# A new issue order for two Sobel layers, and the centring of recurrent weights spread one step to a pair

## The chip, the cores and the metric

The kernel runs on one core of a Trainium2 chip. The core has five engines that run side by side, each with its own queue of instructions that it takes strictly in order: TensorE (PE, matrix products), VectorE (DVE), ScalarE (ACT), GpSimd (POOL) and SyncE (SP, which here only issues transfers). An instruction waits at the head of its queue until semaphores say that what it needs is there. The metric is the device time of one execution in microseconds (us); the median of several executions counts.

## The reference

The input is one image of 256 x 256 pixels with 32 channels, and four layers follow each other, each of the form x = x + f(GroupNorm(x)), with 16 groups over the whole image:

1. an attention over an axis of length one, so that its softmax is 1 and only value, gate and output projection count;
2. and 3. a Sobel layer: a 3x3 mean of the normalized image with zero padding, divided by the number of pixels in the window, then the two Sobel gradients of it, and their magnitude;
4. two recurrent cells over the 256 columns, with a group norm in each step.

```python
pooled = _avg_pool3_same(x)
grad_x = _depthwise3(pooled, kx)
grad_y = _depthwise3(pooled, ky)
return jnp.sqrt(grad_x * grad_x + grad_y * grad_y + EPSILON)
```

Layers 2 and 3 are what the change is about. The recurrent layer comes in through its weights, which are prepared while the Sobel layers run.

## The kernel before

**Layout.** The image lies in SBUF twice, as `xa` and `xb`, each of 128 partitions (4 columns x 32 channels) by 64 blocks by 256 rows. Two blocks make a pair: 128 x 512 numbers. There are 32 pairs (`NST`). A layer reads one image and writes the other, pair by pair.

**One pair of a Sobel layer** (`sobel_layer`, from L382). Work along the free axis (the image's rows) is done by VectorE and GpSimd; work across columns, which means across partitions and neighbouring blocks, is done by matrix products with constant matrices.

- `convert` (L407, ACT, twice): the normalized pair, once into PSUM (`xp`) and once into SBUF (`xn`).
- `twos` (L412, DVE): u, the sum of neighbours, from `xn` and `xp`. `ends` (L417, ACT): the two border values of `pp`, from u times 1.5. `threes` (L422, DVE): the rest of `pp`, the sum of three, from u (SBUF) and `xp` (PSUM). `pp` has two buffers.
- `fours` (L426, DVE): v, the sum of `pp` and `pp` shifted by one. Both operands lie in SBUF.
- `difference` (L435, POOL): dh, `pp` minus `pp` shifted by two. `smooth` (L431, POOL): sh, the sum of v and v shifted by one. Both go into rings of eight blocks (four pairs), since the products need the neighbouring pairs as well.
- `mixed` (L439, PE, twice): for dh and for sh, four products into PSUM, two on each half of the columns; the pair before and the pair after are needed.
- `square` (L473, ACT, twice), `total` (L479, DVE: ss), `root` (L483, ACT), `residual` (L487, DVE: adds the magnitude to the layer's input and writes its output), `statistics` (L490, DVE: bn_stats of the output, for the next group norm).

**What sets the order.** The order of issue is written out by hand. The list `parts` (L494) gives each operation a time within its pair, in units of its own; pair k is moved by k times `every` (L493). All operations of all pairs are sorted by that number and issued in this order (`todo`, L512 to L518). So the numbers decide the order in each engine's queue, and nothing else: when an instruction really runs is up to the queues and semaphores. In steady state, VectorE's queue holds for each pair k: u(k), residual(k-4), statistics(k-4), pp(k), ss(k-3), v(k). ScalarE's: ends(k), the two squares of pair k-3, the two conversions of pair k+1, root(k-3). GpSimd's: dh(k), sh(k). PE's: the products of dh and then those of sh, two pairs behind.

**The work in between.** After each `statistics`, one function of a list is called (L519). In the first Sobel layer the list comes from `centring` (L612): the recurrent weights and biases get their means subtracted. That is two reductions on VectorE for the biases (`bm`), one scaling, eight subtractions on GpSimd (`bc`, L629), then four reductions for the weights (`wm`), one scaling and sixteen subtractions (`wc`): 32 steps. L634 binds them two and two, so that the first 16 pairs take them all. In the second layer the list comes from `products` (L636): a transposition with its copy on ScalarE, two copies on GpSimd, two additions into the biases on VectorE (L651) behind a matrix product each, and an output matrix `e4` with copies on ScalarE and an addition on GpSimd (L666). It has five steps and is not edited.

**Around the layers.** Between the layers the statistics are gathered and turned into a scale and a bias (`group_norm`). After the second Sobel layer the recurrence starts (from 631 us in the profile); SP loads its first inputs `xt` from `xa` as soon as the Sobel buffers are free.

Of the kernel before, what the change touches and what calls it, by code (L numbers as in the profile page):

```python
# [60 lines left out]
def net_kernel(  # L61
# [320 lines left out]
    def sobel_layer(src, dst, scale, bias, between):  # L382
# [107 lines left out]
        def statistics(k):  # L490
            nc.vector.bn_stats(stats[:, k, :], pair(dst, k))  # L491

        every = 3.65  # L493
        parts = [  # L494
            (-1.19, convert, ("xp",)),
            (-0.74, convert, ("xn",)),
            (0.00, twos, ()),
            (0.52, ends, ()),
            (1.98, threes, ()),
            (3.36, difference, ()),  # L500
            (3.62, fours, ()),
            (5.32, smooth, ()),
            (8.70, mixed, (1,)),
            (9.90, mixed, (0,)),
            (12.45, square, (1,)),
            (12.47, square, (0,)),
            (13.90, total, ()),
            (14.41, root, ()),
            (15.59, residual, ()),
            (16.31, statistics, ()),  # L510
        ]
        todo = [  # L512
            (k * every + when, k, part, args) for k in range(NST) for when, part, args in parts
# [8 lines left out]
        return stats  # L522

    stats = sobel_layer(xa, xb, *gn, rw.centring())
    with tc.tile_pool(name="ps_n", bufs=1, space=PSUM) as ps_n:
        gn = group_norm(stats, ps_n, 3, 12)
    stats = sobel_layer(xb, xa, *gn, rw.products())
    second.close()

# [39 lines left out]
class RecurrentWeights:  # L569
# [42 lines left out]
    def centring(self):  # L612
        nc = self.nc
        out = []
        for mean, t in (
            (self.bm, self.bc.rearrange("p l (g m) -> p (l g) m", g=4)),
            (self.wm, self.wc.rearrange("p l k (g m) -> p (l k g) m", g=4)),
        ):
            n = mean.shape[1]
            for i in range(0, n, 4):  # L620
                out.append(
                    lambda mean=mean, t=t, i=i: nc.vector.tensor_reduce(
                        mean[:, i : i + 4], t[:, i : i + 4, :], AX.X, ALU.add
                    )
                )
            out.append(lambda mean=mean: nc.vector.tensor_scalar_mul(mean, mean, 1.0 / H))
            for i in range(n):
                out.append(
                    lambda mean=mean, t=t, i=i: nc.gpsimd.tensor_scalar(  # L629
                        t[:, i, :], t[:, i, :], mean[:, i : i + 1], None, ALU.subtract  # L630
                    )
                )

        return [lambda ps, p=out[i : i + 2]: [f() for f in p] for i in range(0, len(out), 2)]  # L634

    def products(self):  # L636
        nc = self.nc
# [87 lines left out]
class RecurrentInputs:  # L725
# [33 lines left out]
    def of(self, t, rows):  # L759
# [20 lines left out]
        i=10.749, m=14.225, sq=14.912, rd=15.578, pw=16.964, si=17.174, so=17.198, tg=17.865,  # L780
# [3 lines left out]
        i=17.550, m=17.552, sq=18.681, rd=19.727, pw=20.540, si=20.935, sf=21.284, fc=21.803,  # L784
# [289 lines left out]
```

## Time and profile before

| what | us |
|---|---|
| median of 3 runs (2635.06 to 2637.7) | 2635.57 |
| the profiled execution's own time | 2633.51 |
| its span, first to last instruction | 2631.7 |
| first Sobel layer, first u to last statistics | 327.78 to 471.09 |
| second Sobel layer, likewise | 477.20 to 619.46 |
| first products of the recurrence | 631.3 |
| busy in the span: PE, DVE, ACT, POOL | 2553.0, 2348.0, 2291.8, 1273.7 |
| granted TensorE clock, mean | 0.991 |

The span of the profiled execution is 1.8 us shorter than its own time, and that is 2.1 us under the median. Almost nine tenths of the span belong to the recurrence and the first layer, so shares over the whole span say little about the Sobel layers; what they are worth is read from their own stretch. Rows of the timeline give start, duration, engine, line, operation, output from input, shape and count, and in brackets how long the engine had been idle and what ended that. Instructions of one engine may overlap a little: the next one on VectorE starts about 0.07 us before the one in front of it ends, so periods are counted from start to start. Rows of groups give the number of instructions, busy time, the mean duration in ns, and the idle time before them with its releasers.

### The profile page before, as it was taken

To read this page: it belongs to the slowest core of one execution; us is meant where nothing else is said; L and a number is where in the kernel's file an instruction comes from. 1 tells how busy PE (TensorE), PEld (TensorE's weight loads), DVE (VectorE), ACT (ScalarE), POOL (GpSimd) and SP (SyncE) were. 2 spreads that over 40 slices of the span, in tenths; PEclk is the share of its full clock that TensorE was granted. 3 is DMA by queue.
4 is the path that set the end of the run, shared out by engine and by line. 5 is a ranking of instruction groups with operands and counts; after the bars stand their busy time and mean duration, and the time that the engine had idled before them with its cause. 6 is when DMAs were issued, how large, how long until landed. Compare 5 with 4: busy or idle time off the path is not lost.

```text
span 2631.7 us, 43547 instructions
## 1 busy us (share of the span) xinstructions
PE 2553.0 (97%) x11453; PEld 1004.5 (38%) x11453; DVE 2348.0 (89%) x6735; ACT 2291.8 (87%) x6948; POOL 1273.7 (48%) x1288
## 2 busy tenths in 40 slices
PE   7999988987999999999999999999999999999997
PEld 4433433433333333333333333333333333333332
DVE  6788799896999999999999999999999999999996
ACT  5677677675999999999999999999999999999996
POOL 2211265442555555555555555555555555555553
PEclk9899999998999999999999999999999999999998
DMA  4000000002010000001010101010000001000000
GB/s 146 1 1 1 18 1 1 1 1 49 1 24 9 18 12 14 16 10 20 6 21 5 21 5 21 5 24 9 18 11 15 16 10 20 6 5 5 5 5 10
DMA packets 110745, 38.71 MB, mean 15 GB/s; under 512 B 74852, under 2 KB 107653, under 8 KB 110488
## 3 DMA queue, kind: packets, MB, share of 16 engines
q1 hardware_dynamic: 108452, 34.54, 6.1%
q8 instruction: 94, 1.54, 0.2%
q14 instruction: 163, 1.34, 0.2%
q10 hardware_dynamic: 1236, 0.99, 0.1%
q0 software_dynamic: 800, 0.30, 0.1%
HBM read 10.63 MB, written 8.39 MB: 7 GB/s over the span
## 4 chain that ended last, share of the span: by engine, by line
PE 86%; DVE 9%; ACT 2%; issue 1%; DMA 1%; POOL 1%; SPq 0%; DVEq 0%; ACTq 0%; POOLq 0%
PE zz L892 35%; PE zz L887 17%; PE zz L860 8%; PE pt L944 6%; PE pv L315 5%; PE zz L857 3%; DVE v L429 3%; PE pt L940 2%; PE pg L339 2%; DVE stats L491 2%; DVE u L415 1%; PE px L989 1%; PE pg L315 1%; DVE pp L424 1%; PE pc L259 1%
## 5 line engine op out<-in xcount | busy, mean ns | idle before, releaser
L908 POOL TENSOR_TENSOR rs<-ve,mhalf 128x4 f32<-128x4 f32 x1024 | 1046.9, 1022 | 954.6 <-DVE ve L905 954.6
L892 PE MATMUL zz<-wc,hT 128*128 128x512 f32 x2040 | 1068.7, 611 | 1.4 <-DVE hT L950 1.2
L881 ACT ACTIVATE ga<-zz,rs 128x128 f32<-128x128 f32 x3072 | 974.6, 376 | 53.0 <-POOL rs L908 46.3
L905 DVE TENSOR_REDUCE ve<-sq 128x4 f32<-128x516 f32 x1024 | 704.9, 688 | 68.0 <-ACT sq L900 47.4
L900 ACT ACTIVATE sq<-zz 128x512 f32<-128x512 f32 x1024 | 623.8, 609 | 52.2 <-PE zz L892 14.2
L887 PE MATMUL zz<-wc,hT 128*128 128x512 f32 x1024 | 524.1, 594 | 0.0
L892 PEld LDWEIGHTS zz<-wc,hT 128*128 128x128 f32 x2040 | 306.4, 189 | 356.1 <-DVE hT L950 167.5
L881 ACT ACTIVATE go<-zz,rs 128x128 f32<-128x128 f32 x1024 | 394.1, 385 | 0.0
L928 DVE TENSOR_TENSOR c<-ga 128x128 f32<-128x128 f32 x1024 | 298.2, 291 | 64.5 <-ACT ga L881 58.0
L932 DVE TENSOR_TENSOR fc<-ga,c 128x128 f32<-128x128 f32 x1020 | 297.9, 292 | 5.6 <-ACT ga L881 4.1
L936 DVE TENSOR_TENSOR c<-c,fc 128x128 f32<-128x128 f32 x1020 | 286.6, 281 | 8.8
L860 PE MATMUL zz<-fx,xt 32*128 32x512 f32 x2048 | 265.7, 588 | 0.0
L471 PE MATMUL pg<-dh,kt 128*64 128x512 f32 (+1 forms) x584 | 175.8, 544 | 24.9 <-POOL dh L437 24.6
L333 DVE TENSOR_TENSOR o<-pv,sg 128x512 f32<-128x512 f32 x256 | 158.0, 680 | 42.3 <-PE pg L315 37.7
L940 PEld LDWEIGHTS pt<-ident,go 128*128 128x128 f32 x512 | 71.1, 139 | 290.2 <-ACT go L881 282.7
L887 PEld LDWEIGHTS zz<-wc,hT 128*128 128x128 f32 x1024 | 172.6, 208 | 9.4 <-issue 9.4
L944 PEld LDWEIGHTS pt<-ident,c 128*128 128x128 f32 x512 | 71.1, 139 | 268.2 <-DVE c L936 260.1
L947 ACT ACTIVATE th<-c 128x128 f32<-128x128 f32 x512 | 165.9, 324 | 4.4 <-DVE c L936 1.2
L944 PE MATMUL pt<-ident,h 128*128 128x128 f32 x512 | 157.5, 308 | 10.4 <-DVE h L954 8.1
L330 ACT ACTIVATE sg<-pg 128x512 f32<-128x512 f32 x256 | 138.6, 599 | 30.0 <-PE pg L315 25.3
L947 ACT ACTIVATE th<-pt 128x128 f32<-128x128 f32 x512 | 146.3, 286 | 18.9 <-PE pt L944 18.9
L950 DVE TENSOR_TENSOR hT<-pt,th 128x128 f32<-128x128 f32 x512 | 144.1, 281 | 13.7 <-ACT th L947 13.7
(161 smaller groups left out, 3006.0 us busy)
## 6 DMA issues: line engine op xcount, KB each, us to landing
xt<-xa SPq DMA_DIRECT2D x256, 64.0 KB, 2.0
nat<-in_x_dram SPq DMA_DIRECT2D x16, 512.0 KB, 7.8
out_dram<-st SPq DMA_DIRECT2D x252, 32.0 KB, 1.7
wc<-in_L_conv_W_cell_dram SPq DMA_DIRECT2D x2, 512.0 KB, 5.0
kt<-in_consts_dram ACTq DMA_DIRECT2D x1, 832.0 KB, 5.8
wv<-in_L_conv_Wv_dram POOLq DMA_DIRECT2D x4, 32.0 KB, 5.0
wg<-in_L_conv_Wg_dram POOLq DMA_DIRECT2D x4, 32.0 KB, 6.7
out_dram<-st ACTq DMA_DIRECT2D x4, 32.0 KB, 3.8
```

The costliest lines, as they stand in the source:

```text
L860: nc.tensor.matmul(v["zz", l, h, t], lhsT=inputs.of(t, r), rhs=fx[r, :], start=False, stop=l == 0 and t == 0,)
L881: nc.scalar.activation(dst, gates(x, g), func, scale=scale)
L887: nc.tensor.matmul(get("zz"), lhsT=v["hT", 0, t][:, seqs], rhs=wc[:, l, 0, :], start=False, stop=t == 0)
L892: nc.tensor.matmul(get("zz"), lhsT=v["hT", l, t - 1][:, seqs], rhs=wc[:, l, 1, :], start=False, stop=True,)
L900: nc.scalar.activation(sqs[l, h][:, :, 0:H], four(get("zz")), AF.Square, scale=float(H**-0.5))
L905: nc.vector.tensor_reduce(ve, sqs[l, h], AX.X, ALU.add)
L908: nc.gpsimd.tensor_tensor(rs, get("ve"), inputs.mhalf, ALU.pow)
L928: nc.vector.tensor_mul(c, gates(get("ga"), 0), gates(get("ga"), 2))
L932: nc.vector.tensor_mul(fc, gates(get("ga"), 1), get("c"))
L936: nc.vector.tensor_add(c, c, get("fc"))
L944: nc.tensor.transpose(get("pt")[:, 1, 0:P], get("c" if turned else "h"), ident)
L947: nc.scalar.activation(th, get("pt")[:, 1, 0:P] if turned else get("c"), AF.Tanh)
```

## The change

Two edits. The list of times in `sobel_layer` gets other numbers. In steady state they give this order for pair k. VectorE: u(k), residual(k-4), pp(k), statistics(k-4), v(k), ss(k-3). ScalarE: ends(k), the two squares of pair k-3 in the other order (that of sh first), conversions of pair k+1, root(k-3). GpSimd: sh(k-1), the step in between if there is one, dh(k); in its queue that is dh and sh by turns as before. PE: the products of sh for pair k-2, then those of dh for pair k-1, by turns as before, those of dh one pair earlier. The work in between stands where statistics stands: now between statistics and v on VectorE, and between sh(k-1) and dh(k) on GpSimd. Which instruction waits for which result is as before. At a layer's start, where there is no residual and no statistics yet, v follows directly on pp, as before; only the fourth v now stands ahead of the first ss.

The second edit takes the steps of `centring` one by one: 32 steps for 32 pairs, the last of them after the last statistics.

```diff
-        every = 3.65
+        every = 3.55
         parts = [
-            (-1.19, convert, ("xp",)),
-            (-0.74, convert, ("xn",)),
+            (-2.19, convert, ("xp",)),
+            (-2.05, convert, ("xn",)),
             (0.00, twos, ()),
-            (0.52, ends, ()),
-            (1.98, threes, ()),
-            (3.36, difference, ()),
-            (3.62, fours, ()),
-            (5.32, smooth, ()),
-            (8.70, mixed, (1,)),
-            (9.90, mixed, (0,)),
-            (12.45, square, (1,)),
-            (12.47, square, (0,)),
-            (13.90, total, ()),
-            (14.41, root, ()),
-            (15.59, residual, ()),
-            (16.31, statistics, ()),
+            (0.23, ends, ()),
+            (1.36, threes, ()),
+            (2.12, fours, ()),
+            (2.54, difference, ()),
+            (4.61, smooth, ()),
+            (6.40, mixed, (1,)),
+            (8.63, mixed, (0,)),
+            (11.70, square, (0,)),
+            (11.94, square, (1,)),
+            (12.98, total, ()),
+            (14.18, root, ()),
+            (14.75, residual, ()),
+            (16.24, statistics, ()),
         ]
...
-        return [lambda ps, p=out[i : i + 2]: [f() for f in p] for i in range(0, len(out), 2)]
+        return [lambda ps, f=f: f() for f in out]
```

## Prediction

> **What bounds the kernel now.** I read the groups of instructions first, for what the Sobel layers' operations cost; then busy time by stretches, for the engine that bounds these layers; then the timeline of a few pairs, for the order of events; last the layer's end, where one chain stands bare.
>
> ```profile
> L429 DVE TENSOR_TENSOR v<-pp 128x514 f32<-128x514 f32 x64 | 74.3, 1161 | 0.7
> L437 POOL TENSOR_TENSOR dh<-pp 128x512 f32<-128x512 f32 x64 | 72.0, 1125 | 91.2 <-ACT xp L410 69.8 <-DVE pp L424 15.5 <-PE pg L471 5.9
> L433 POOL TENSOR_TENSOR sh<-v 128x512 f32<-128x512 f32 x64 | 66.4, 1038 | 37.5 <-DVE v L429 29.8 <-PE pg L471 7.6
> ...
> 520.00:560.00 40.00, 36.01 (x169) 12.95 (x167) 39.66 (x57) 29.43 (x57) 19.74 (x19) 1.00 0.00 1
> ```
>
> The sum v takes 1.16 us where VectorE's other operations of this size (u, pp, ss) take 0.67 to 0.68. The last row (columns PE, PEld, DVE, ACT, POOL) is from the middle of the second Sobel layer: VectorE is busy 39.66 of 40 us, PE 36.0 with overlaps counted, ScalarE 29.4, GpSimd 19.7. VectorE bounds both layers. One period of its work, in the timeline:
>
> ```profile
> 543.44 0.67 DVE L424 TENSOR_TENSOR pp<-u,xp 128x508 f32<-128x508 f32 x1
> ...
> 544.02 0.68 DVE L481 TENSOR_TENSOR ss<-sq,pg 128x512 f32<-128x512 f32 x1
> ...
> 544.28 1.04 POOL L437 TENSOR_TENSOR dh<-pp 128x512 f32<-128x512 f32 x1 [1.49 <-ACT xp L410]
> ...
> 544.62 1.25 DVE L429 TENSOR_TENSOR v<-pp 128x514 f32<-128x514 f32 x1
> ...
> 545.79 0.67 DVE L415 TENSOR_TENSOR u<-xn,xp 128x510 f32<-128x510 f32 x1
> ...
> 546.02 1.04 POOL L433 TENSOR_TENSOR sh<-v 128x512 f32<-128x512 f32 x1 [0.70 <-PE pg L471]
> ...
> 546.39 0.67 DVE L488 TENSOR_TENSOR xa<-xb,pg 128x512 f32<-128x512 f32 x1
> ...
> 547.10 0.69 DVE L491 BATCH_NORM_STATS2 stats<-xa 128x6 f32<-128x512 f32 x1
> ...
> 547.71 0.67 DVE L424 TENSOR_TENSOR pp<-u,xp 128x508 f32<-128x508 f32 x1
> ```
>
> From start to start: pp 0.58, ss 0.60, v 1.17, u 0.60, residual 0.71 (statistics wait for its result), statistics 0.61: 4.27 us a pair. The difference dh starts 0.84 after pp's start, that is as soon as pp is there; v comes 0.34 later, and ends 0.55 after dh does (545.87 against 545.32). So v waits for dh: 0.57 us a pair. At the layer's end nothing covers the chain from total over root to residual:
>
> ```profile
> 613.86 0.67 DVE L481 TENSOR_TENSOR ss<-sq,pg 128x512 f32<-128x512 f32 x1
> 614.57 0.69 ACT L485 ACTIVATE pg<-ss,sobel_eps 128x512 f32<-128x512 f32 x1 [1.07 <-DVE ss L481]
> ...
> 615.29 0.69 DVE L488 TENSOR_TENSOR xa<-xb,pg 128x512 f32<-128x512 f32 x1 [0.76 <-ACT pg L485]
> ```
>
> It is 1.43 us from ss to residual. In the old order v, u and 0.60 more lie between them (544.02 to 546.39, 2.37), so it costs nothing.
>
> **What the Trainium skill says.** "SBUF — State Buffer", section "Who interferes with whom": a VectorE instruction with two SBUF inputs contends with a GpSimd instruction that reads SBUF, whoever is first blocks the other, one with at most one SBUF input doesn't, and tensor_reduce never does. The trace agrees: v alone of these operations reads two SBUF operands, and v alone is stretched; u lies beside sh and takes 0.67. Of a tensor_reduce beside dh no row of before shows anything.
>
> **The change, step by step.** In steady state VectorE's new order is ss, u, residual, pp, statistics, v. dh still waits for pp, for the scaled ends on ScalarE and for an old ring slot on PE, all as before; on GpSimd's queue it still stands between the last pair's sh and its own, with at most one centring in front. Its being issued after v in the program doesn't hold it back, for v is on another queue. One period, with ss at 0:
> - u at 0.60. root at 0.71, residual at 1.43: only u lies between now, so VectorE waits 0.23 for ScalarE.
> - pp at 2.03 (0.60 on). Statistics at 2.62 (0.59); the residual is done by then, so the old 0.11 for it goes. v is issued at 3.23.
> - dh at pp + 0.84 = 2.87, to 3.91. v starts 0.36 after it, waits, ends at 3.91 + 0.55 = 4.46; the next ss starts 0.08 before that (545.79 against 545.87), at 4.38.
>
> With ss and root at 0.68 and 0.69 while other engines run, I take 4.39, against 4.27: +0.12. From the fifth pair on 27 periods in each layer: 54 x 0.12 = +6.5 us.
>
> Others follow. ScalarE (some 3.1 of 4.39), PE (two steps of 0.43 for each of four groups, 3.4) and GpSimd (1.04 + 1.04 + 0.60 for one centring) fit into the period. Had they not, their excess would be added in full.
> - The six means of the centring (reductions, 0.67) stood before pp and cost 0.59 each from start to start, the two scalings 0.08: 3.7. Now they stand between statistics and v: v is issued 0.59 later, ends at pp + 2.47 instead of 2.44, so each costs 0.04. But in the pair behind the first two, v took 0.68 before, which saved 0.57. Net 0.24 - 3.7 + 0.57 = -2.9. If a reduction doesn't overlap with dh this is zero.
> - Centring one to a pair: GpSimd had 0.34 idle even behind two (1.19), so nothing is won on the path. Four are left to the layer's last pairs, behind the last sh, where GpSimd has 4 us free; layer 2 needs them some 20 us later.
> - The layer's start: the first root is ready early, -0.2 in each.
> - Layer 2's products. Before, the six periods from u at 488.07 took 1.95 more than 6 x 4.27. After: the copy of the transposed weights now precedes root on ScalarE and waits for PE one group longer, +0.7; the two additions into bc, between statistics and v, cost 0.1 each; the addition into e on GpSimd now stands ahead of dh and waits for ScalarE's copies, so one v is free of dh (-0.6) and one partly (-0.3). Together about 0, so -2.0 (this takes in the start).
> - The tail: the last residuals start behind u + 4.39 + 0.83 instead of u + 4.27 on, +0.95 a layer.
>
> Layer 1: 3.2 - 2.9 - 0.2 + 0.95 = +1.0. Layer 2: 3.2 - 2.0 + 0.95 = +2.1. The recurrence, from 631 us on, is untouched; the loads of xt on SP (29 issued in 18.8 us, the first 16 needed by 631) start when PE lets go of the ring, move with the tail, and have 5 us to spare. No DMA changes its place. Sum +3.0 us: 2633.5 for the profiled execution becomes 2636.5, and the median of 2635.57, 0.08% above it, becomes 2638.6.
>
> **Rivals.** First, v gets ahead of dh. Three of the 64 pairs show it:
>
> ```profile
> 505.64 1.93 POOL L437 TENSOR_TENSOR dh<-pp 128x512 f32<-128x512 f32 x1 [1.89 <-DVE pp L424]
> 505.99 0.68 DVE L429 TENSOR_TENSOR v<-pp 128x514 f32<-128x514 f32 x1
> ```
>
> v starts 0.35 after dh, takes 0.68, and dh is stretched by 0.9 instead. These are the pairs with 0.353 to 0.355 between the starts; in those where v waits it is at most 0.347. The new order gives about 0.36. For: the distance. Against: a later start is an odd reason to win; all three stand right behind VectorE instructions on 33 partitions (the bm reductions, the additions into bc), which the normal pair has not; and in two pairs v started 0.05 after dh and waited the longest (1.54). If v wins everywhere, the period is 4.38 - 0.55 = 3.83, GpSimd (1.93 + 1.04 + 0.60 = 3.57) still fits: 54 x -0.44 = -23.8; the credit of the reductions goes (+0.6 against before), the products cost +0.5, tails +0.4 each, start -0.2: about -22, 2613.5. In layer 2 alone, where no centring shifts dh: about -10.
>
> Second, slower: the wait of residual for root. It stands on VectorE's queue ahead of pp, statistics and v, so PE and GpSimd get their inputs late with it. I have 0.24 a pair. The change is slower by over 0.2% (5.3 us) once it is 0.04 wider, since 54 x 0.043 = 2.3. ScalarE's root has the ends behind it and the conversions before it; if root starts 0.1 late in each pair, +5.4: 2644. Against: ScalarE idles a microsecond before root.
>
> Third, the change doesn't do what it says (v still beside dh): that is my forecast.
>
> **From cases to numbers.** v still waits for dh with the sum as worked out: 0.55, 2633 to 2644, of which 0.40 within 0.2%, 0.13 above, 0.02 below. v ahead, in both layers or one: 0.25. Wider wait, or credits that fail: 0.20. So faster 0.27, same 0.40, slower 0.33; 0.2% is about what a measurement of this kernel can tell from no change. The range runs from the first rival's time to just past the second's, 2612 to 2646.
>
> **What would show it.** v with a mean near 1.2 us, and dh at 1.04 beside it; an idle time before the residual of over 0.2 a pair released by root; 4.39 between two pp; reductions directly before v, with v near 0.7 there. A v of 0.68 with a dh of 1.93 in most pairs makes the first rival right, an idle time of 0.3 or more the second. The forecast falls too if tensor_reduce is stretched beside dh.

## The result, and the profile after

The changed kernel takes 2641.82 us (median; 2638.98 to 2645.66), the kernel before 2635.36 beside it (2634.1 to 2637.7). The ratio is 1.0024, interval 1.0014 to 1.0034: slower by 0.24%, or 6.5 us. 2638.6, 3.0 us more than the kernel before, was forecast.

| us | before | after | difference | forecast |
|---|---|---|---|---|
| first Sobel layer | 143.32 | 144.93 | +1.61 | +1.0 |
| second Sobel layer | 142.26 | 145.85 | +3.58 | +2.1 |
| from the second layer's end on | 2012.22 | 2014.66 | +2.4 | 0 |
| span of the profiled execution | 2631.7 | 2640.0 | +8.3 | +3.0 |

(The rest of the span differs by +0.7: -0.2 before the first layer, +0.84 between the two.) First the groups of the changed kernel, and its row for the middle of the second layer (columns PE, PEld, DVE, ACT, POOL):

```profile
L437 POOL TENSOR_TENSOR dh<-pp 128x512 f32<-128x512 f32 x64 | 70.8, 1106 | 94.5 <-DVE pp L424 54.8 <-ACT xp L410 19.2 <-PE pg L471 17.4
L429 DVE TENSOR_TENSOR v<-pp 128x514 f32<-128x514 f32 x64 | 69.0, 1078 | 0.9
...
520.00:560.00 40.00, 38.12 (x174) 14.65 (x170) 38.53 (x56) 29.79 (x55) 18.82 (x19) 1.00 0.00 1
```

v still takes 1.08 us on average, and VectorE, which had been busy for 39.66 of the 40 us from 520 to 560, now has 1.5 of them without work. It does 56 instructions there; before it did 57. One period of the timeline says why:

```profile
537.05 0.68 DVE L424 TENSOR_TENSOR pp<-u,xp 128x508 f32<-128x508 f32 x1
...
537.64 0.69 DVE L491 BATCH_NORM_STATS2 stats<-xa 128x6 f32<-128x512 f32 x1
537.89 1.04 POOL L437 TENSOR_TENSOR dh<-pp 128x512 f32<-128x512 f32 x1 [1.63 <-DVE pp L424]
...
538.24 1.24 DVE L429 TENSOR_TENSOR v<-pp 128x514 f32<-128x514 f32 x1
539.40 0.67 DVE L481 TENSOR_TENSOR ss<-sq,pg 128x512 f32<-128x512 f32 x1
...
540.00 0.67 DVE L415 TENSOR_TENSOR u<-xn,xp 128x510 f32<-128x510 f32 x1
540.11 0.69 ACT L485 ACTIVATE pg<-ss,sobel_eps 128x512 f32<-128x512 f32 x1 [1.14 <-DVE ss L481]
...
540.84 0.69 DVE L488 TENSOR_TENSOR xa<-xb,pg 128x512 f32<-128x512 f32 x1 [0.16 <-ACT pg L485]
...
541.44 0.68 DVE L424 TENSOR_TENSOR pp<-u,xp 128x508 f32<-128x508 f32 x1
```

v starts 0.35 us behind dh, as before, and ends 0.55 behind its end (539.48 against 538.93), as before. What is new is the mark at the residual: VectorE idles for 0.16 there and waits for root. From u to residual it is 0.84, where 0.60 would do. From pp to pp it is 4.39; over many pairs the period is 4.40, against 4.27.

The end of the second layer, in the same view:

```profile
622.49 0.67 DVE L481 TENSOR_TENSOR ss<-sq,pg 128x512 f32<-128x512 f32 x1
623.19 0.69 ACT L485 ACTIVATE pg<-ss,sobel_eps 128x512 f32<-128x512 f32 x1 [1.07 <-DVE ss L481]
623.91 0.69 DVE L488 TENSOR_TENSOR xa<-xb,pg 128x512 f32<-128x512 f32 x1 [0.76 <-ACT pg L485]
```

The chain that nothing covers is what it was, 1.42 from ss to residual; but the residuals of the last four pairs now begin later behind the last u, and from that u to the layer's end it is 14.94 us instead of 13.95.

From the second layer's end on, both kernels issue the same instructions, and no difference was forecast; the trace has +2.4. It goes with the clock that TensorE was granted, 0.9893 of full speed in the profiled execution after, 0.9909 before. In both traces this clock is either full or half, and the half comes in stretches of 3.41 us or a multiple. Compared with the kernel before, the changed kernel has one such stretch less behind the second layer, one more at the recurrence's start, and one more in the last 23 us. If the same ScalarE instructions are followed in both traces from the second layer's end, the changed kernel is ahead by 1.5 us after the first of these places and behind by 0.4 or 0.5 after the second. From there it wanders between 0.2 ahead and 1.0 behind, is 0.4 behind after 1985 us, and 1.8 at ScalarE's last instruction. So the difference arises at these places and doesn't grow along the recurrence. The +0.84 between the layers looks the same: 3.3 of its 6.11 us before, and 5.0 of 6.95 after, are at half clock, and the group norm's small products stand on PE behind filler products (`junk`, L145) that take 0.63 us each at half clock and 0.38 at full.

Among all executions, those with a clock of 0.991 have a mean span of 2637.2 after (one execution) and 2632.2 before, those with 0.990 2638.8 and 2633.8, those with 0.989 2640.7 and 2635.0 (before: the 31 executions that ran beside the first eight experiments). At an equal clock the change costs 5.0 to 5.7 us, which fits the two Sobel layers' 5.2. The last microsecond or so of the 6.5 then goes with the lower mean clock, 0.9894 against 0.9901. Whether the change lowers the clock or these ten executions met it by chance is open. Against the change speaks that seven further executions of the kernel before, beside the last experiments, have 0.9894 too, and that the old order with one step of centring to a pair (one_a_pair_old_order below) also has 6.9 us between the layers, while the new order with ss moved (total_first) has 6.1.

### The profile page after: what moved, and what is told of

Same layout as the page of the kernel before. It is cut to its first block, busy times and chain, and to the rows that moved or that the text cites. A ratio compares the mean times of both kernels' runs of the same rounds, so it can differ in the third digit from the quotient of the medians.

```text
span 2640.0 us, 43662 instructions
## 1 busy us (share of the span) xinstructions
PE 2569.7 (97%) x11453; PEld 1001.3 (38%) x11453; DVE 2344.3 (89%) x6735; ACT 2294.7 (87%) x6948; POOL 1272.0 (48%) x1288
## 3 DMA queue, kind: packets, MB, share of 16 engines
q8 instruction: 94, 1.54, 0.2%
## 4 chain that ended last, share of the span: by engine, by line
PE 88%; ACT 5%; DVE 4%; issue 1%; DMA 1%; POOL 1%; SPq 0%; DVEq 0%; ACTq 0%; POOLq 0%
PE zz L892 35%; PE zz L887 17%; PE zz L860 8%; PE pt L944 6%; PE pv L315 5%; PE zz L857 3%; PE pt L940 2%; PE pg L339 2%; PE pg L471 2%; DVE v L429 2%; ACT xp L410 1%; PE px L989 1%; ACT pg L485 1%; PE pg L315 1%; DVE ss L481 1%; PE pc L259 1%
## 5 line engine op out<-in xcount | busy, mean ns | idle before, releaser
L471 PE MATMUL pg<-dh,kt 128*64 128x512 f32 (+1 forms) x584 | 160.1, 549 | 15.4 <-POOL dh L437 8.9
L471 PE MATMUL pg<-sh,kt 128*64 128x512 f32 (+1 forms) x584 | 157.9, 541 | 0.0
```

Of the source, the lines that this page charges most:

```text
L471: nc.tensor.matmul(dst, lhsT=w, rhs=rhs, start=first, stop=not side)
```

## The experiments

The layers' lengths below come from one profiled execution of each kernel. Two pairs of kernels have the same instructions in the same order in the first layer; their lengths differ by 0.1 us or less (144.93 and 144.83 for the changed kernel and biases_split, 126.10 and 126.10 for total_first and total_first_split).

### Is v's wait for dh the price, and is VectorE the bound?

The theory: both orders lose 0.57 us in each pair because v meets dh, the new one loses 0.24 more to root, and with v out of the way VectorE sets the period. Four kernels test it, each the changed kernel with one operation cut down or moved.

**tiny_dh**: dh is issued at its place but writes two columns, so the kernel leaves out nearly all of the horizontal differences (the ring is set to zero once, ahead of each layer).

```diff
-            nc.gpsimd.tensor_sub(along[1][:, ring(k), :], pp[:, :, 0:S], pp[:, :, 2 : S + 2])
+            nc.gpsimd.tensor_sub(along[1][:, ring(k), 0:1], pp[:, :, 0:1], pp[:, :, 2:3])
```

> The new order; dh is cut to two columns of 512 on GpSimd (the rest of the ring stays zero), so that the horizontal differences are left out and only the time of dh is taken away. Theory (v is stretched by waiting for dh): v takes 0.68 in all pairs, the period falls from 4.40 by 0.57 to 3.83 and the gap before the residual stays at 0.24; first layer about 133.5, second about 132. Rival (v is slow by itself once statistics stand ahead of it): v stays at 1.25, both layers stay at 145 to 146.

Measured: period 3.83, layers 131.78 and 132.07 us, 2612.81 us in one execution. The group of v:

```profile
L430 DVE TENSOR_TENSOR v<-pp 128x514 f32<-128x514 f32 x64 | 43.5, 680 | 1.0
```

The wait of 0.57 a pair is all dh's, and the 0.24 in front of the residual stays: 3.83 is six VectorE operations at 0.60 and that gap. (The first layer is 1.7 us shorter than expected. The trace has 0.57 of it at each of the two scalings of the centring, which in the changed kernel wait for dh too, as shown further down, and 0.5 in the fourth period.)

**total_first**: ss ahead of v.

```diff
-            (12.98, total, ()),
+            (12.73, total, ()),
```

> The new order with total (ss) moved ahead of v, so that VectorE does pp, statistics, ss, v. Then v is issued 1.80 us after pp, dh ends 1.89 after it[...]; and v and u lie between ss and the residual, 1.8 against the 1.43 that root needs. Theory (v waits for dh, the residual for root): both waits go, v takes 0.68, the period falls from 4.40 to about 3.61. Each reduction costs its 0.59 again. First layer about 127, second about 126, in all about 2604 us. Rival (v is slow for another reason than dh, as its two operands in SBUF or its width): v stays at 1.25 and the period at 4.2, about 2630 us. Second rival (PE with 3.41 a pair or its latency takes over as the bound): v at 0.68 but a period of 3.8 or more, VectorE waiting for squares.

Measured: 2602.07 us, ratio 0.988 (0.9863 to 0.9896) to the kernel before; layers 126.10 and 127.59. Its timeline:

```profile
526.10 0.67 DVE L424 TENSOR_TENSOR pp<-u,xp 128x508 f32<-128x508 f32 x1
...
526.70 0.68 DVE L491 BATCH_NORM_STATS2 stats<-xa 128x6 f32<-128x512 f32 x1
...
526.95 1.04 POOL L437 TENSOR_TENSOR dh<-pp 128x512 f32<-128x512 f32 x1 [0.78 <-ACT pg L477]
527.30 0.67 DVE L481 TENSOR_TENSOR ss<-sq,pg 128x512 f32<-128x512 f32 x1
...
527.89 0.68 DVE L429 TENSOR_TENSOR v<-pp 128x514 f32<-128x514 f32 x1
```

One place later in the queue, v starts 0.94 behind dh and is not stretched, though dh runs for another 0.10: it ends 0.58 behind dh, and a v that waits ends 0.55 behind it. ss, which reads PSUM for one operand, lies beside dh at no cost. And since v and u now stand between ss and residual, root is covered as well. The period is 3.58, six operations at 0.60, with no gap, as the row for 40 us in the second layer shows (columns as above):

```profile
520.00:560.00 40.00, 39.96 (x206) 21.58 (x203) 40.00 (x68) 35.64 (x68) 23.47 (x23) 1.00 0.00 1
```

VectorE sets the pace, but PE is not far from it: its eight steps of 0.43 make 3.4 us a pair. One number in the list decides some 40 us.

**v_behind_pp**: statistics behind v, so that v follows directly on pp and comes before dh.

```diff
-            (16.24, statistics, ()),
+            (16.36, statistics, ()),
```

> The new order with statistics behind v, so that v follows directly on pp. It then is issued 0.79 us after pp, and dh starts 0.85 after pp: v should be first, as in the first pairs of each layer, where it starts 0.04 to 0.07 ahead of dh, takes 0.70, and dh takes 1.5. Theory: v at 0.70, dh at 1.52, the gap before the residual stays at 0.24, a period of 4.03, first layer about 138, second about 137.5, in all about 2627 us. Rival (0.05 us is too little and dh is first): v takes 1.5, the period is 4.8 and the time about 2660 us.

Measured: 2628.4 us, ratio 0.9973 (0.9964 to 0.9983), period 4.06.

```profile
540.21 0.68 DVE L424 TENSOR_TENSOR pp<-u,xp 128x508 f32<-128x508 f32 x1
...
541.02 0.69 DVE L429 TENSOR_TENSOR v<-pp 128x514 f32<-128x514 f32 x1
541.06 1.56 POOL L437 TENSOR_TENSOR dh<-pp 128x512 f32<-128x512 f32 x1 [1.51 <-DVE pp L424]
```

v is 0.04 ahead and keeps its 0.69; dh waits instead, and GpSimd has the time. v itself starts 0.81 behind pp, since it needs pp finished, and root's 0.24 remains. So the period is 0.34 shorter than after, and not 0.57.

**stats_later**: the same, with statistics a pair later, between u and residual, and the work in between moved to follow the residual.

```diff
-            (16.24, statistics, ()),
+            (18.25, statistics, ()),
...
-                if part is statistics and between:
+                if part is residual and between:
```

> As the one with v directly behind pp, and statistics moved one pair later, between u and the residual (the work in between now follows the residual). This fills the gap that waits for root. Theory: v at 0.70 and no idle time of VectorE before the residual; a period of 0.60 + 0.60 + 0.60 + 0.60 + 0.79 + 0.60 = 3.80 us; about 2614 us. The difference to the run with v behind pp alone, 0.23 a pair, is what the gap costs. Rival (the gap isn't a wait for root, or root moves later with it): a period of 4.03 as in that run.

Measured: 2614.16 us, ratio 0.9926 (0.9909 to 0.9942), period 3.80. Of the gaps in v_behind_pp only the one between pp and v is left (0.81 instead of 0.60). The four periods, 3.58, 3.80, 3.83 and 4.06, each 0.03 or less from what was expected, are accounted for by VectorE's operations and waits; no other bound shows in the steady state.

### What is the second edit worth?

**two_a_pair** is the changed kernel with the old return line of `centring`, as in this diff; **one_a_pair_old_order** is the kernel before with the reverse of it.

```diff
-        return [lambda ps, f=f: f() for f in out]
+        return [lambda ps, p=out[i : i + 2]: [f() for f in p] for i in range(0, len(out), 2)]
```

> The new order with the centring bound two and two as it was. Theory (the new order costs the time: v still waits for dh, and a gap before the residual; the spread of the centring is worth little): pairs without a step keep a period of 4.40 us in both layers. In the two pairs with two reductions only the first hides behind dh, so each costs 0.59 more: the first Sobel layer takes 146.1 (144.9 with single steps), the second 145.9 as in the changed kernel. Rival (the single steps of the centring, each beside a pair, are what costs): the first layer comes back to 143.3, its length in the kernel before.

> The old order with the centring one step to a pair: the second edit alone. Theory: nothing on the path changes; each reduction still costs its 0.59 ahead of pp, GpSimd had 0.34 us idle even behind two steps. First layer 142.7 to 143.9 (143.3 before; the spread because of single pairs in which v is ahead of dh), second 142.3, the time within 1 us of the kernel before. Rival (spreading the steps costs by itself): first layer over 144.5.

Measured: two_a_pair 2643.26 us (ratio to before 1.0034, 1.0021 to 1.0046), first layer 146.62, second 146.06. one_a_pair_old_order 2635.73 (1.000, 0.9991 to 1.0008), first layer 142.33, second 141.99. By the first layer's length, spreading the centring saves 1.7 us in the new order and 1.0 in the old one, where the least expected length was 142.7. In the whole time 1 us can't be told from nothing: the time of one_a_pair_old_order is that of before. So the loss is the new order's, and by the layers' lengths the second edit gives a little of it back.

The 1.0 in the old order is mostly not time that the centring itself takes. One more pair in which v gets ahead of dh gives 0.57. Another 0.29 comes from a dh that starts 0.3 us later than usual behind pp (1.13 to 1.16 instead of 0.84), so that v waits 1.54. Such a dh stands in the 17th pair of the first layer and in the 15th of the second, in all five kernels with the centring two and two, and in none of the eight with single steps. The second layer, whose work in between isn't edited, is shorter for it by 0.27 in one_a_pair_old_order, and longer by 0.21 in two_a_pair. What delays it isn't shown.

### Where does the second layer lose more than forecast?

In the changed kernel's trace, around the first of the two additions into `bc`:

```profile
501.69 1.04 POOL L437 TENSOR_TENSOR dh<-pp 128x512 f32<-128x512 f32 x1 [1.62 <-DVE pp L424]
...
502.20 1.02 PE L650 MATMUL pg<-wc,latt 128*33 128x512 f32 x2
503.26 0.68 DVE L651 TENSOR_TENSOR bc<-bc,pg 33x512 f32<-33x512 f32 x1 [1.13 <-PE pg L650]
503.87 0.68 DVE L429 TENSOR_TENSOR v<-pp 128x514 f32<-128x514 f32 x1
```

The addition waits 1.13 us for its product, and v is queued behind it; the second addition waits 0.75. In the kernel before, each had waited 0.43, here the first:

```profile
499.37 0.68 DVE L651 TENSOR_TENSOR bc<-bc,pg 33x512 f32<-33x512 f32 x1 [0.43 <-PE pg L650]
```

The product is issued in the same step, and PE takes it behind the products of the Sobel pairs ahead of it (they end at about 502.4). That is the order that the Trainium skill states in "PSUM — Partial Sum Buffer", section "Engine vs sequencer instructions": matrix products start and complete in program order. This trace agrees.

**biases_split** issues each product one step ahead of its addition.

```diff
-        def biases(ps, l):
-            pf = ps()[0:KX, :]
-            nc.tensor.matmul(pf, lhsT=self.latt, rhs=self.wc[:, l, 0, :], start=True, stop=True)
-            nc.vector.tensor_add(self.bc[:, l, :], self.bc[:, l, :], pf)
+        def product(ps, l):
+            pf[l] = ps()[0:KX, :]
+            nc.tensor.matmul(pf[l], lhsT=self.latt, rhs=self.wc[:, l, 0, :], start=True, stop=True)
+        def biases(ps, l):
+            nc.vector.tensor_add(self.bc[:, l, :], self.bc[:, l, :], pf[l])
...
-            lambda ps: biases(ps, 0),
-            lambda ps: biases(ps, 1),
+            lambda ps: product(ps, 0),
+            lambda ps: [biases(ps, 0), product(ps, 1)],
+            lambda ps: biases(ps, 1),
```

> The new order; in the second layer each product for the biases is issued one pair ahead of the addition that reads it, the rest is the same. Theory (the additions, now between statistics and v, wait for PE, and these two waits are what the second layer lost over the forecast): VectorE's idle time of 1.13 and 0.75 ahead of the two additions goes, v in these two pairs hides what is left behind dh, the second layer takes 143.9 (145.85 in the changed kernel). Rival (PE is late in these pairs anyway, its queue being full): the same wait shows up at the squares or one pair later, and the second layer stays at 145.5 or more.

Measured: the two periods with additions fell from 5.66 and 5.28 to 4.42 and 4.42, against a steady 4.40. With no wait for PE, each addition costs 0.02, because it hides beside dh. But the layer takes 145.09, not 143.9. The step behind, with the output matrix `e4`, stands one pair later now, and took back 1.4: two periods that had been 3.83 and 3.83 became 3.82 and 5.24. Its own trace has there:

```profile
519.01 0.74 ACT L669 COPY e<-pg 32x32 f32<-32x32 f32 x4 [1.20 <-PE pg L660]
519.66 0.68 ACT L485 ACTIVATE pg<-ss,sobel_eps 128x512 f32<-128x512 f32 x1
...
520.38 0.69 DVE L488 TENSOR_TENSOR xa<-xb,pg 128x512 f32<-128x512 f32 x1 [1.57 <-ACT pg L485]
```

The residual waits 1.57 us for root, root stands on ScalarE behind the four copies of `e4`, and these have waited 1.20 for a matrix product. One wait was removed and the next one grew. In all it took 2643.58 us in one execution, at a granted clock of 0.988, so its whole time says nothing about 0.7 us. The expected cause is shown, for both waits are gone; that the layer gets all of it back is not.

**total_first_split** takes this edit over into total_first.

> The order of total_first together with the additions of biases_split. In total_first the two periods with the additions take 6.23 and 5.28 against 3.58. With the products a pair ahead each addition should cost only its own 0.60, since in this order nothing hides it: 2.65 + 1.70 - 1.20 = 3.15 less; the output's step, which cost 0.72 more in biases_split than it did in the changed kernel's place, may take 1 back. Second Sobel layer 124.5 to 125.5 (127.6 in total_first), 2599 to 2600 us in all. Rival: the waits for PE only move to the next step, and the layer stays at 127 or more.

Measured: 2600.69 us, ratio to the kernel before 0.9864 (0.9848 to 0.9881); second layer 126.10, 1.5 less than in total_first, between what was expected and the rival. The periods with the additions are 4.18, the steady 3.58 plus 0.60 for the addition, since in this order nothing hides it. The output's step again took 1.5 back (3.66 and 5.86 where total_first had 3.58 and 4.41). It is the fastest kernel here; its lead of 1.4 us over total_first is not settled by these few executions.

### Which of the two gets ahead?

In three pairs of the kernel before, v went first although dh had started 0.35 earlier. Two things marked them: the largest distances, and VectorE instructions on 33 partitions just ahead of pp. **few_partitions** is the kernel before with one such instruction in each pair, whose result nobody uses; **few_128** has it on all partitions, **few_short** on 33 but over a quarter of the length.

```diff
+        few = kp.tile([P, 4], F32, name="few")
...
+                if part is statistics:
+                    nc.vector.tensor_reduce(few[0:33], kt[0:33, 0:4, :], AX.X, ALU.add)
```

few_128 has `few` and `kt[:, 0:4, :]` in it, few_short `few[0:33, 0:1]` and `kt[0:33, 0:1, :]`.

> The old order with one more instruction in each pair, directly ahead of pp: a reduction of 33 partitions x 512 constants into a tile that nobody reads. It is to tell what let v get ahead of dh in three of 64 pairs of the kernel before. First theory (an instruction on 33 partitions shortly ahead): v takes 0.68 and dh 1.93 in nearly all pairs, the period is 4.27 + 0.59 - 0.57 = 4.29. Second theory (the distance, 0.353 us or more between the starts of dh and v): it stays near 0.345, so v takes 1.25 in nearly all pairs and the period is 4.86.

> The order of before, with one more tensor_reduce in each pair, ahead of pp. As in few_partitions, but on all 128 partitions instead of 33. If it is the 33 partitions that let v get ahead of the difference there: v waits again, 1.25 us, the difference takes 1.04, and the period is 4.27 + 0.59 = 4.86; about 2635 + 54 x 0.59 = 2667 us. If any reduction ahead of pp does it: v 0.68, the difference 1.93, period 4.29, and about 2643 us as in few_partitions.

> The order of before, with a tensor_reduce on 33 partitions ahead of pp as in few_partitions, but over 128 numbers in a partition instead of 512. If its length does not matter: v 0.68, the difference 1.93, and the instruction costs about 0.15, so the period is 4.27 - 0.57 + 0.15 = 3.85, and the time about 2635 - 54 x 0.42 = 2612 us. If only a long one does it: v 1.25, period 4.42, about 2643 us.

Measured, in one execution each, by groups, first few_partitions (2643.13 us, period 4.29):

```profile
L438 POOL TENSOR_TENSOR dh<-pp 128x512 f32<-128x512 f32 x64 | 116.9, 1827 | 81.3 <-DVE pp L425 65.1 <-ACT xp L411 12.6 <-ACT xn L411 2.2
L430 DVE TENSOR_TENSOR v<-pp 128x514 f32<-128x514 f32 x64 | 44.7, 699 | 0.7
```

then few_128 (2669.45 us, period 4.86):

```profile
L430 DVE TENSOR_TENSOR v<-pp 128x514 f32<-128x514 f32 x64 | 74.3, 1160 | 0.7
L521 DVE TENSOR_REDUCE few<-kt 128x4 f32<-128x512 f32 x64 | 42.8, 669 | 0.0
```

and few_short (2646.4 us, period 4.45):

```profile
L430 DVE TENSOR_TENSOR v<-pp 128x514 f32<-128x514 f32 x64 | 72.3, 1130 | 0.7
L521 DVE TENSOR_REDUCE few<-kt 33x1 f32<-33x128 f32 x64 | 16.6, 260 | 0.0
```

With the long reduction on 33 partitions ahead of pp, v goes first in 54 of 56 pairs (the first four of each layer left out): 0.68, and dh 1.93. The same reduction on 128 partitions, in the same place and of the same duration, leaves v waiting in 52 pairs; in the other four it did not wait in the kernel before either. The short one on 33 partitions leaves it waiting in 50. The distances between the starts as the trace has them (0.34 to 0.35 in all three) don't tell these apart, so the distance theory, on which the first rival rested, falls. That 33 partitions suffice falls as well. few_partitions is no faster for it, since the reduction costs what v gains.

But the short reduction isn't without effect. In few_short, the two pairs with the late dh, where v starts only 0.05 or 0.06 behind it, have v going first:

```profile
542.10 1.65 POOL L438 TENSOR_TENSOR dh<-pp 128x512 f32<-128x512 f32 x1 [1.96 <-DVE pp L425]
542.16 0.68 DVE L430 TENSOR_TENSOR v<-pp 128x514 f32<-128x514 f32 x1
```

In these pairs v waits in the kernel before and in few_128 (1.53 to 1.54). A v that came 0.18 behind its dh (1.40) still waited in few_short. So the reduction on 33 partitions may give v a lead that grows with its length: between 0.06 and 0.18 us with 128 numbers, 0.35 or more with 512. No run tests another length. What gives the lead, with pp and ss between the reduction and v, is open.

## Why the prediction was right in kind and short in size

**The steady state** was right at each step: v starts 0.35 behind dh (0.36 forecast), ends 0.55 behind its end, dh stays at 1.04, the residual waits for root (0.24 from start to start), and the period is 4.40 (4.39). Twenty-seven periods cost 3.8 and 3.6 us a layer; 3.2 was forecast, since 0.01 a pair is 0.3 a layer. Two of the signs that the prediction named by number came out a little lower: v's mean is 1.08 and not near 1.2, since 20 of the 64 don't wait, and the idle time that the trace marks before the residual is 0.16 and not over 0.2.

**The six reductions** stand directly ahead of v, which takes 0.68 there, and cost 0.02 each (0.04). All work in between was to give 2.9 back in the first layer and gave 3.4. Of this, 0.3 is the late dh, which the changed kernel doesn't have; no term of the forecast stood for it.

**The two scalings** cost 0.07 each, near the nothing that was forecast, but not because they are short:

```profile
349.90 0.72 DVE L626 TENSOR_SCALAR bm<-bm 33x8 f32<-33x8 f32 x1
350.53 0.68 DVE L429 TENSOR_TENSOR v<-pp 128x514 f32<-128x514 f32 x1
```

In the kernel before, this scaling takes 0.15. Here it starts 0.35 behind a dh, takes 0.72 and ends 0.02 behind it, so it waits in v's place, and v behind it no longer has to.

**Centring one to a pair** was put at nothing on the path. That was wrong by the length of the layer: 1.7 us (two_a_pair), of which 0.3 is the late dh. The step looked at GpSimd's idle time in the old order. In the new one a single reduction hides beside dh, but two in one pair do not: in two_a_pair that period is 5.02, with one of them it is 4.42. And where two subtractions come late enough to lie beside v, v takes 2.06 and the period 5.22. The total hardly shows this error, since the 0.04 for each reduction had been worked out for one alone in its pair.

**The start** was to save 0.2. The first four periods took 0.4 more in the first layer and 0.2 in the second, and the fifth saved 0.2. A fifth u that waits 0.74 and 0.70 for its conversion had not been seen.

**The products** are the mis-sized term. The step said that the two additions into bc, between statistics and v, cost 0.1 each: it counted the instruction, which does hide, and forgot what it waits for. They cost 1.26 and 0.88. The waiting instruction moved from ahead of pp to ahead of v in VectorE's queue, and in PE's its product stands behind groups that end later, so the wait grew from 0.43 to 1.13 and 0.75. The rest of that step was near: the turn (the transposition and its copy) +0.3 (0.7 forecast), the two periods freed of dh -0.6 each (-0.6 and -0.3). With the start, and with 0.3 for the late dh of this layer, -1.0 instead of -2.0.

**The tail** cost 1.0 in each layer, 0.95 forecast.

The first layer's sum is then 3.8 + 0.2 - 3.4 + 1.0 = +1.6, the second's 3.6 - 1.0 + 1.0 = +3.6. Together the layers gave +5.2 instead of +3.1, still just under 0.2% (5.3 us); the measured 6.5 is beyond it only with what goes with the clock. The forecast had 0.40 on the one and 0.33 on the other. That the first layer came within 0.6 us of its forecast is partly luck, for the late dh made up for part of what the start and the longer period cost.

**The rivals.** v did not get ahead of dh in the steady state, and few_short, where v waits at 0.350 to 0.353, shows that the distance would not have made it so. The wait for root is not wider than worked out, so the second rival's place was right, and its size the forecast's own. The third, that the change leaves v beside dh, is what happened.

The skill's page on SBUF ("SBUF — State Buffer", section "Who interferes with whom") said that a tensor_reduce never contends, and the six reductions beside dh show it, 0.66 to 0.67 each. It says too that issue order decides who blocks, and that the other one is blocked fully. v_behind_pp agrees, with v 0.04 ahead and dh waiting. few_partitions, where the trace has v start later and go first, doesn't, as far as starts in a trace show the order of issue. What the prediction took from the page on instructions with at most one SBUF input leaves out the page's condition: it holds outside the modes that use both pairs of ports, and a tensor_scalar is among the operations that can enter these. The scalings are tensor_scalars, and they waited. Whether they ran in such a mode, no trace shows.

## What to carry to other kernels

When two instructions on different engines shut each other out, as v and dh do here, look for an instruction without that conflict that can be put between them in the queue of the engine that sets the pace; here ss and v changed places and the layers became an eighth shorter than in the changed kernel. Then follow the chain that the exchange shortens or lengthens, as with ss, root and residual, and see what covers it. For each step that is put between, ask not only what it takes but what it waits for and who is queued behind it.

## What the runs showed of the hardware

- Of v and dh, the one that comes second waits for nearly all of the other. v ends 0.55 behind dh's end (0.68 alone); a dh that comes second ends 0.90 behind v's end (1.04 alone), whether it started 0.04 behind v (1.56 in all) or 0.35 before it (1.93).
- A small tensor_scalar on VectorE waits for dh too: the two scalings (33x8 and 128x16 numbers) take 0.15 and 0.17 us in the kernel before, and 0.72 beside dh in the changed one, where they end 0.02 and 0.03 behind its end.
- GpSimd's centring shuts v out as well. In two_a_pair one v takes 2.06 us. It starts beside the second of two subtractions on 33 partitions, dh follows them directly, and v ends 0.55 behind that dh:

```profile
349.36 1.17 POOL L629 TENSOR_SCALAR bc<-bc,bm 33x128 f32<-33x128 f32 x2
...
350.03 2.06 DVE L429 TENSOR_TENSOR v<-pp 128x514 f32<-128x514 f32 x1
350.51 1.03 POOL L437 TENSOR_TENSOR dh<-pp 128x512 f32<-128x512 f32 x1
```

- A tensor_reduce over 512 numbers on 33 partitions, three instructions ahead of v in the queue, made v go before a dh that the trace shows starting 0.34 to 0.35 earlier. On 128 partitions it didn't. With 128 numbers on 33 it did so only where dh had started 0.05 or 0.06 earlier.
